# Residual adds regrouped by step, loads reordered, and the closing check spread over three engines in a chunked recurrence

## The chip, the cores and the metric

The kernel runs on one core of one Trainium2 chip. The metric is the device time of one execution, in microseconds (us). The core has five engines that run side by side and wait for one another through semaphores: PE (matrix products), DVE (element-wise work and reductions), ACT (activation functions), POOL (more element-wise work) and SP (here: only starts transfers). "PEld" is PE's loading of weights. Transfers (DMAs) run on 16 DMA engines that all queues share; nearly all of them are started by SP and belong to the queue q1.

## The reference, cut to what matters

The input is x, 4 batches of 128 channels and 4096 tokens (64 x 64). Layer 0 adds a full attention to x, layer 1 adds a causal attention, and then comes the part that the change touches:

```
Wx = layernorm(t) @ W.T                      # t: 4 x 4096 tokens x 128 channels
Wx = (Wx - mean) * rsqrt(var + eps) * gamma + beta     # mean, var over all 4 x 4096 tokens
y = 0
for n in range(4096):                        # one recurrence along the tokens of a batch
    y = sigmoid(Wx[:, n] + y @ V.T)
    ys[:, n] = y
t = t + ys
```

The result t is returned with channels first.

## The kernel before, in words

**The attention layers** (all but the last 60 us of the span) are not touched by the change. At their end the tensor t of each batch lies in DRAM scratch: x2c holds batches 0 and 1 by channels, x2t holds batches 2 and 3 by tokens. These are the "by-channel" batches (b < BY_C = 2) and the "by-token" batches. The last piece of x2t is written at L872, near the end of the last attention block. The projected inputs Wx of the recurrence lie on the chip in xs.

**The recurrence** is cut into chunks. Each batch's 4096 tokens are split into NCH = 256 chunks of STEPS = 16 tokens, and all 256 chunks of a batch advance together: one state tile has 128 channels on the partitions and 256 chunks along the free axis. A chunk doesn't know the state that it should start from. So it first runs over some tokens of the chunk ahead of it (three early steps inside the attention stage, then WARM = 6 steps numbered -6 to -1), which brings it near the right state; that warmed state is kept in the tile start. Then come the 16 real steps, 0 to 15. So there are 22 rounds of 4 batches in this stage.

**One step of one batch** (function step) is a chain over three engines: a product y_ps = V.T x previous state on PE (L1294, which the profile shows as two MATMULs), an add z = Wx x scale + y_ps on DVE (L1296), and a sigmoid on ACT (L1300) that writes the state. The next step of the same batch needs that state. The four batches are independent of each other, so the engines work on the others while one batch's chain is under way.

**The residual** t + ys is added in two ways:

- By-channel batches: add(s) on POOL (L1307) adds the states of batches 0 and 1 of step s to the tile xc (the reloaded x2c), and SP writes the sum out (L1309, 256 KB, pieces of 1 KB). The tile sum has three buffers.
- By-token batches: residual(s0, b, h) takes four steps of one half of the chunks of one batch. PE transposes the four 128x128 blocks into one PSUM tile yT_ps (L1328), DVE adds it to the tile xr, which is the reloaded x2t, in place (L1333), and SP writes it out (L1334, 256 KB, pieces of 2 KB). There are 16 such groups. Twelve are called inside the loop, one in each step from step 4 on, after batch 1's step. Most of the states that they take there are older than the step just before; only the groups called in steps 4, 8 and 12 also take batch 2's state of the step just before, as their fourth block. Four groups are left for after the loop.

**The closing check** (function meet): the last state of a chunk must agree with the warmed start of the next chunk. PE forms the difference with two products, by the identity and by minus the identity (L1317, L1318), ACT squares it twice and sums along the chunks (L1320, L1321). One such pass is made for each of the 4 batches, interleaved with the four remaining residual groups. Then DVE compares the sums with TOL to the fourth power (L1361), counts (L1362), PE adds the counts over the partitions (L1364), and DVE writes a flag (L1367). All engines read the flag (L1424) and branch (L1425): if a check failed, a slow general path would run. With these inputs it doesn't. After the branch SP waits for the landing of all its transfers, and the program ends.

**The order of the work.** A scheduler orders each engine's instructions by when it estimates them to be ready. pin(instruction) (keep_in_program_order) forbids that for one instruction: it comes after whatever the program issued on the same engine just ahead of it. In the kernel before, the step's instructions are pinned from step 4 on, of a residual group the first transpose, the DVE add and the output transfer are pinned, and the loads of xc and xr are not. On each engine instructions start in that order.

**The loads** of this stage are issued on SP: first xc in 8 DMAs of 512 KB (L1249), then xr in 4 DMAs of 1 MB (L1259). xr is read from step 4 on, a quarter of it (one batch, one half) for each group; xc from step 0 on, all 8 parts for each sum.

**PSUM.** Each batch has one buffer for its products (ps_y), and the transposed groups have four (ps_r). [...]

Of the kernel before, what the change touches and what calls it, by code (L numbers as in the profile page):

```python
# [9 lines left out]
F32 = mybir.dt.float32  # L10
AF = mybir.ActivationFunctionType
# [349 lines left out]
def fast_path(  # L361
# [878 lines left out]
    with tc.tile_pool(name="xr", bufs=1) as xrp, tc.tile_pool(name="y", bufs=2) as yp, tc.tile_pool(  # L1240
        name="sums", bufs=3
    ) as sums, tc.tile_pool(
        name="ps_r", bufs=4, space=PSUM
    ) as ps_r, tc.tile_pool(name="ps_y", bufs=1, space=PSUM) as ps_y:

        xc = xrp.tile([P, BY_C, NCH, STEPS], F32, name="xc")
        for b in range(BY_C):
            for c in range(Q):
                nc.sync.dma_start(  # L1249
                    out=xc[ts(c, S), b].rearrange("r (g k) s -> r g (k s)", g=NB),  # L1250
                    in_=x2c[b, :, :, c].rearrange("g r n -> r g n"),
                )
# [4 lines left out]
        for b in range(B - BY_C):  # L1257
            for h in range(HALVES):
                nc.sync.dma_start(out=xr[:, b, h], in_=by_chunk(x2t)[b, h])  # L1259
# [12 lines left out]
        assert HALVES * TPB == NB  # L1272
# [3 lines left out]
        def states(b, s):  # L1276
            if b < BY_C:
                return by_step[:, b, s]
            return pair(early[:, b - BY_C, s]) if s < TPB else late[:, b, s // TPB - 1, s % TPB]

        def step(b, s):
# [4 lines left out]
            order = pin if s >= TPB else lambda ins: None  # L1286
# [25 lines left out]
        gap = xrp.tile([P, B], F32, name="gap")  # L1312

        def meet(b):
            ps = ps_y.tile([P, NCH], F32, tag=f"y{b}", name="gap_ps")
            shaped = grid if b < BY_C else pair
            pin(nc.tensor.matmul(shaped(ps), lhsT=ident, rhs=prev[b], start=True, stop=False))  # L1317
            nc.tensor.matmul(ps, lhsT=minus, rhs=start[:, b, 1:], start=False, stop=True)  # L1318
            sq = yp.tile([P, NCH], F32, tag=f"y{b}", name="sq")
            nc.scalar.activation(sq, ps, AF.Square)  # L1320
            nc.scalar.activation(sq, sq, AF.Square, accum_out=gap[:, b : b + 1])  # L1321


        def residual(s0, b, h):

            ps = ps_r.tile([P, TPB, P], F32, tag="r", name="yT_ps")
            for j in range(TPB):
                ins = nc.tensor.transpose(ps[:, j], states(b, s0 + j)[:, h], ident)  # L1328
                if not j:
                    pin(ins)  # L1330
            part = ds(s0, TPB)
            t = xr[:, b - BY_C, h, part]
            pin(nc.vector.tensor_tensor(t, t, ps, ALU.add))  # L1333
            pin(nc.sync.dma_start(out=by_chunk(out_t)[b - BY_C, h, :, part], in_=t))  # L1334


        groups = [(s0, b, h) for s0 in range(0, STEPS, TPB) for b in range(BY_C, B) for h in range(HALVES)]
        assert HALVES * (B - BY_C) == TPB
        for s in range(-WARM, STEPS):
            for b in range(B):  # L1340
                step(b, s)
                if b == 1 and s >= TPB:
                    group = groups.pop(0)
                    residual(*group)
            if 0 <= s < STEPS - 1:
                add(s)
        tc.mark_branch_hint_location(BRANCH, "LikelyTaken", engines=mybir.ALL_ENGINES)
        for k, group in enumerate(groups):
            residual(*group)
            if k == 1:  # L1350
                add(STEPS - 1)
            if k:
                meet(k - 1)
        meet(B - 1)
# [4 lines left out]
        def judge():  # L1359
            total = xrp.tile([P, 1], F32, name="total")  # L1360
            tc.keep_in_program_order(nc.vector.tensor_scalar(count[:, :B], gap, TOL**4, None, ALU.is_le))  # L1361
# [70 lines left out]
```

## Time and profile before

| what | us |
|---|---|
| median of the 3 timed runs (2019.7 to 2020.23) | 2019.79 |
| the profiled execution, its own time | 2020.46 |
| its span, first to last instruction | 2018.7 |
| first product of the recurrence's 22 rounds (L1294) | from 1961.60 |
| transposes of the first residual group (L1328) | from 1981.97 |
| end of the last sigmoid (L1300) | 2008.75 |
| the comparison that closes the check (L1361) | 2014.47 |
| end of the flag (L1367) | 2015.36 |
| last issue of an output transfer (L1334) | 2012.50 |

The page of the profile gives busy times and the chain that ended last for the whole span; the attention layers fill 97% of it. What the change touches lies in the last 60 us, so the views to read are the timeline and the chain in order of time for that window. In a line of the timeline, the first number is the start in us, the second how long the group of instructions lasts from its first start to its last end, then come engine, source line, operation, out<-in and the shape, a count, and in brackets the idle time ahead of it with what ended it. Ends of MATMULs are modelled by the profiler. A line of the chain in order of time has the start, the time that the chain spent there, and the engine, tile and line.

### The profile page before, as it was taken

The numbers are of one execution on the slowest core, as the hardware profiler recorded it, in microseconds if no ns is written. First come the engines' busy times: TensorE is split into PE (matmuls) and PEld (weight loads), VectorE is DVE, ScalarE is ACT, GpSimd is POOL, SyncE is SP. The second block draws the span as 40 slices with busy tenths as digits, with TensorE's granted clock in tenths as the row PEclk, the third lists the DMA queues.
The fourth block names the chain that finished last, engine by engine and source line by source line (L and its number), as shares of the span: only waits on it lengthen the run. The fifth ranks groups of instructions, "written<-read, shape, count | busy, mean of one in ns | idle before, by whom it ended". The sixth has DMA issues, their size and how long they took to land.

```text
span 2018.7 us, 31252 instructions
## 1 busy us (share of the span) xinstructions
PE 2008.4 (99%) x11888; PEld 876.3 (43%) x11888; DVE 1455.7 (72%) x2811; ACT 975.5 (48%) x1057; POOL 139.8 (7%) x238
## 2 busy tenths in 40 slices
PE   9999999999999999999999999999999999999998
PEld 3333354444333345444433334444433333544457
DVE  4799977554789987655588997655478898764568
ACT  4666633333666653333366664333356665333247
POOL 1000011000000001000000001000000000110014
PEclk9999999999999999999999999999999999999999
DMA  3111112220110111330112111231010111120038
GB/s 105 44 33 23 22 33 50 61 53 16 43 49 18 23 23 37 74 69 16 43 21 60 23 19 32 53 79 37 16 43 2 23 22 23 33 53 16 16 78 278
DMA packets 238443, 89.02 MB, mean 44 GB/s; under 512 B 174816, under 2 KB 219360, under 8 KB 237776
## 3 DMA queue, kind: packets, MB, share of 16 engines
q1 hardware_dynamic: 237280, 86.42, 18.1%
q8 instruction: 94, 1.54, 0.3%
q14 instruction: 61, 0.50, 0.1%
q0 software_dynamic: 288, 0.39, 0.1%
q10 hardware_dynamic: 720, 0.16, 0.0%
HBM read 45.84 MB, written 36.89 MB: 41 GB/s over the span
## 4 chain that ended last, share of the span: by engine, by line
PE 97%; DVE 2%; ACT 1%; issue 0%; POOL 0%; POOLq 0%; DVEq 0%; ACTq 0%
PE s_ps L1017 23%; PE acc L1075 22%; PE s_ps L1004 22%; PE acc L1066 22%; PE o_ps L673 1%; PE kr_ps L562 1%; PE r_ps L624 1%; PE wx_ps L938 1%; DVE z L1296 1%; PE v_ps L574 1%; PE o_ps L685 1%; PE y_ps L1294 1%; DVE xr L1333 0%; PE warm_ps L524 0%; ACT xs L1300 0%; ACT p L1011 0%
## 5 line engine op out<-in xcount | busy, mean ns | idle before, releaser
L1046 DVE TENSOR_TENSOR dsum<-dsum,p 128x1024 f32<-128x1024 f32 x692 | 845.4, 1222 | 403.1 <-ACT p L1020 295.3
L1011 ACT ACTIVATE p<-s_ps,nshift 128x1024 f32<-128x1024 f32 x512 | 569.6, 1116 | 312.9 <-PE s_ps L1004 295.5
L1020 ACT ACTIVATE p<-s_ps 128x1024 f32<-128x1024 f32 (+2 forms) x288 | 274.2, 952 | 601.8 <-PE s_ps L1017 576.7
L1066 PE MATMUL acc<-p,v 64*64 64x512 f32 x4096 | 530.0, 589 | 0.0
L1004 PE MATMUL s_ps<-kr,swap 64*64 64x512 f32 x2048 | 524.6, 590 | 1.3 <-ACT p L1011 1.3
L1004 PE MATMUL s_ps<-kr 64*64 64x512 f32 x2048 | 522.3, 590 | 0.0
L1017 PE MATMUL s_ps<-rows,xhT 128*128 128x512 f32 (+3 forms) x1152 | 500.7, 558 | 0.0
L1075 PE MATMUL acc<-p,xh 128*128 128x512 f32 (+3 forms) x1152 | 500.2, 557 | 0.0
L1017 PEld LDWEIGHTS s_ps<-rows,xhT 128*128 128x128 f32 x1152 | 214.9, 190 | 244.8 <-issue 202.9
L1075 PEld LDWEIGHTS acc<-p,xh 128*128 128x128 f32 x1152 | 216.1, 190 | 239.8 <-issue 223.4
L1066 PEld LDWEIGHTS acc<-p,v 64*64 64x64 f32 x4096 | 156.9, 133 | 283.2 <-issue 274.8
L1004 PEld LDWEIGHTS s_ps<-kr,swap 64*64 64x64 f32 x2048 | 141.8, 133 | 145.7 <-issue 136.0
L1004 PEld LDWEIGHTS s_ps<-kr 64*64 64x64 f32 x2048 | 141.5, 133 | 135.6 <-issue 134.1
L713 POOL TENSOR_TENSOR ln_rstd<-ln_var,mhalf 128x4 f32<-128x4 f32 x64 | 69.9, 1092 | 1186.0 <-DVE ln_var L711 1186.0
L1054 DVE TENSOR_TENSOR dsum<-dsum,p 128x256 f32<-128x256 f32 (+1 forms) x120 | 56.2, 501 | 60.0 <-POOL p L1026 60.0
L699 DVE SCALAR_TENSOR_TENSOR xs<-o_ps,recs,xs 128x128 f32<-128x128 f32 x256 | 70.5, 343 | 5.4 <-PE o_ps L685 1.7
L729 DVE TENSOR_SCALAR xh<-xs,ln_mv,ln_rstd 128x128 f32<-128x128 f32 x252 | 70.2, 342 | 1.9
L708 DVE BATCH_NORM_STATS2 ln_st<-xs 128x6 f32<-128x128 f32 x256 | 62.8, 272 | 0.0
L1026 POOL TENSOR_SCALAR_AFFINE_SELECT p<-p 128x128 f32<-128x128 f32 x128 | 34.5, 294 | 351.9 <-ACT p L1020 347.7
L1044 DVE COPY dsum<-p 128x1024 f32<-128x1024 f32 x44 | 30.2, 686 | 24.7 <-ACT p L1020 15.2
L743 DVE STREAM_TRANSPOSE sqT<-xh 128x512 f32<-128x512 f32 x63 | 44.7, 710 | 1.7
L943 ACT COPY xs<-wx_ps 128x512 f32<-128x512 f32 x31 | 18.1, 584 | 50.4 <-DVE stats L939 48.4
(161 smaller groups left out, 898.3 us busy)
## 6 DMA issues: line engine op xcount, KB each, us to landing
xs<-in_xT SPq DMA_DIRECT2D x32, 256.0 KB, 3.2
by_r<-sqT SPq DMA_DIRECT2D x128, 64.0 KB, 2.2
xhT<-by_r SPq DMA_DIRECT2D x128, 64.0 KB, 2.0
by_c<-sqT SPq DMA_DIRECT2D x124, 64.0 KB, 1.8
xhT<-by_c SPq DMA_DIRECT2D x31, 256.0 KB, 2.8
xs<-in_x SPq DMA_DIRECT2D x12, 512.0 KB, 5.4
swap<-kr SPq DMA_DIRECT2D x32, 128.0 KB, 2.3
x2c<-sqT SPq DMA_DIRECT2D x64, 64.0 KB, 2.3
```

What stands on the lines that cost most here:

```text
L699: nc.vector.scalar_tensor_tensor(t, in0=op[:, ts(j, P)], scalar=rec[:, j : j + 1], in1=t, op0=ALU.mult, op1=ALU.add)
L708: nc.vector.bn_stats(st[:, j], xs[:, b, ds(g * BLK + j * P, P)])
L713: nc.gpsimd.tensor_tensor(y, var, mhalf, ALU.pow)
L729: nc.vector.tensor_scalar(dst[:, j], xs[:, b, ds(g * BLK + j * P, P)], mv[:, j, 0:1], y[:, j : j + 1], ALU.subtract, ALU.mult)
L1004: nc.tensor.matmul(ps[c * M : c * M + M, ts(r, BLK)], lhsT=keys[:, ts(c, M)], rhs=rows[r], start=True, stop=True,)
L1011: nc.scalar.activation(it.p, ps, AF.Exp, bias=nshift)
L1017: nc.tensor.matmul(ps[:, off : off + n], lhsT=lhsT, rhs=rhs, start=True, stop=True)
L1020: ins = nc.scalar.activation(it.p[:, :off], ps[:, :off], AF.Exp, scale=float(P) ** -0.5)
L1046: nc.vector.tensor_tensor(flat, flat, it.p, ALU.add)
L1054: nc.vector.tensor_tensor(den[:, h, q0:], den[:, h, q0:], it.p[:, o : o + n], ALU.add)
L1066: nc.tensor.matmul(bt.acc[c * M : c * M + M, r], lhsT=bt.v[part, m * TPB + j, h], rhs=it.p[part, ts(c, BLK)], start=it.first, stop=it.last,)
L1075: ins = nc.tensor.matmul(bt.acc[:, 0, q0:], lhsT=bt.xh[:, t], rhs=it.p[:, o : o + n], start=it.first and h == 0, stop=it.last and h == 1,)
```

## The change

- xr is loaded ahead of xc, and both sets of loads are pinned.
- A residual group is now one step of both by-token batches and both halves: four transposes (batch 2 half 0, batch 2 half 1, batch 3 half 0, batch 3 half 1) of step s into one PSUM tile, one DVE add of the same size as before, and two output transfers of 128 KB (one per batch) in pieces of 512 bytes. Group s-1 is called in step s, after batch 1's step, from step 1 on. Fifteen groups lie inside the loop and one after it.
- The step's instructions are pinned from step 1 on.
- ps_r has three buffers; the freed PSUM bank holds the new tile met. In steps 4 and 5 ACT copies the warmed starts of batches 2 and 3 into it.
- The check is shared: batches 0 and 1 get their difference from PE, batches 2 and 3 from a DVE subtraction (away); the fourth powers of batches 0 and 3 are summed on ACT, the largest absolute differences of batches 1 and 2 are found on DVE. The comparison is made with the tile tol, which holds TOL to the fourth power or TOL.

```diff
@@ -1240,23 +1240,25 @@
     with tc.tile_pool(name="xr", bufs=1) as xrp, tc.tile_pool(name="y", bufs=2) as yp, tc.tile_pool(
         name="sums", bufs=3
     ) as sums, tc.tile_pool(
-        name="ps_r", bufs=4, space=PSUM
-    ) as ps_r, tc.tile_pool(name="ps_y", bufs=1, space=PSUM) as ps_y:
-
-        xc = xrp.tile([P, BY_C, NCH, STEPS], F32, name="xc")
-        for b in range(BY_C):
-            for c in range(Q):
-                nc.sync.dma_start(
-                    out=xc[ts(c, S), b].rearrange("r (g k) s -> r g (k s)", g=NB),
-                    in_=x2c[b, :, :, c].rearrange("g r n -> r g n"),
-                )
+        name="ps_r", bufs=3, space=PSUM
+    ) as ps_r, tc.tile_pool(name="ps_m2", bufs=1, space=PSUM) as ps_m2, tc.tile_pool(name="ps_y", bufs=1, space=PSUM) as ps_y:
 
         HALVES = NCH // P
         by_chunk = lambda t: t.rearrange("b (h q s) c -> b h q s c", q=P, s=STEPS)
         xr = xrp.tile([P, B - BY_C, HALVES, STEPS, P], F32, name="xr")
         for b in range(B - BY_C):
             for h in range(HALVES):
-                nc.sync.dma_start(out=xr[:, b, h], in_=by_chunk(x2t)[b, h])
+                pin(nc.sync.dma_start(out=xr[:, b, h], in_=by_chunk(x2t)[b, h]))
+
+        xc = xrp.tile([P, BY_C, NCH, STEPS], F32, name="xc")
+        for b in range(BY_C):
+            for c in range(Q):
+                pin(
+                    nc.sync.dma_start(
+                        out=xc[ts(c, S), b].rearrange("r (g k) s -> r g (k s)", g=NB),
+                        in_=x2c[b, :, :, c].rearrange("g r n -> r g n"),
+                    )
+                )
 
         mv = xrp.tile([P, nc.vector.BN_AGGR_DIM], F32, name="mv")
         nc.vector.bn_aggr(mv, ends)
@@ -1269,7 +1271,7 @@
 
-        assert HALVES * TPB == NB
+        assert HALVES * TPB == NB and HALVES * (B - BY_C) == TPB
         early = xrp.tile([P, B - BY_C, TPB, NCH], F32, name="early")
         late = xs.rearrange("p b (r h k q) -> p b k r h q", h=HALVES, r=TPB, q=P)
 
@@ -1283,7 +1285,7 @@
             wx = by_step[:, b, s % STEPS]
             shaped = (lambda t: t) if s < 0 else grid if b < BY_C else pair
 
-            order = pin if s >= TPB else lambda ins: None
+            order = pin if s >= 1 else lambda ins: None
             if s == -1:
                 y = start[:, b, 1:]
             elif s < 0:
@@ -1309,56 +1311,72 @@
             tc.keep_in_program_order(nc.sync.dma_start(out=out_c[:, :, s].rearrange("b c k -> c b k"), in_=t))
 
-        gap = xrp.tile([P, B], F32, name="gap")
-
-        def meet(b):
-            ps = ps_y.tile([P, NCH], F32, tag=f"y{b}", name="gap_ps")
-            shaped = grid if b < BY_C else pair
-            pin(nc.tensor.matmul(shaped(ps), lhsT=ident, rhs=prev[b], start=True, stop=False))
-            nc.tensor.matmul(ps, lhsT=minus, rhs=start[:, b, 1:], start=False, stop=True)
-            sq = yp.tile([P, NCH], F32, tag=f"y{b}", name="sq")
-            nc.scalar.activation(sq, ps, AF.Square)
-            nc.scalar.activation(sq, sq, AF.Square, accum_out=gap[:, b : b + 1])
-
-        def residual(s0, b, h):
+        def residual(s):
 
             ps = ps_r.tile([P, TPB, P], F32, tag="r", name="yT_ps")
             for j in range(TPB):
-                ins = nc.tensor.transpose(ps[:, j], states(b, s0 + j)[:, h], ident)
+                ins = nc.tensor.transpose(ps[:, j], states(BY_C + j // HALVES, s)[:, j % HALVES], ident)
                 if not j:
                     pin(ins)
-            part = ds(s0, TPB)
-            t = xr[:, b - BY_C, h, part]
-            pin(nc.vector.tensor_tensor(t, t, ps, ALU.add))
-            pin(nc.sync.dma_start(out=by_chunk(out_t)[b - BY_C, h, :, part], in_=t))
-
-        groups = [(s0, b, h) for s0 in range(0, STEPS, TPB) for b in range(BY_C, B) for h in range(HALVES)]
-        assert HALVES * (B - BY_C) == TPB
+            t = xr[:, :, :, s]
+            pin(nc.vector.tensor_tensor(t, t, ps.rearrange("p (b h) c -> p b h c", h=HALVES), ALU.add))
+            for b in range(B - BY_C):
+                pin(nc.sync.dma_start(out=by_chunk(out_t)[b, :, :, s].rearrange("h q c -> q h c"), in_=t[:, b]))
+
+        met = ps_m2.tile([P, BY_C, NCH], F32, name="met")
+        gap = xrp.tile([P, B], F32, name="gap")
+        tol = xrp.tile([P, B], F32, name="tol")
+        nc.gpsimd.memset(tol, TOL)
+        nc.gpsimd.memset(tol[:, 0:1], TOL**4)
+        nc.gpsimd.memset(tol[:, B - 1 :], TOL**4)
+
         for s in range(-WARM, STEPS):
             for b in range(B):
                 step(b, s)
-                if b == 1 and s >= TPB:
-                    group = groups.pop(0)
-                    residual(*group)
+                if b == 1 and s >= 1:
+                    residual(s - 1)
+            if TPB <= s < TPB + BY_C:
+                b = s - TPB
+                pin(nc.scalar.copy(met[:, b], start[:, BY_C + b, 1:]))
             if 0 <= s < STEPS - 1:
                 add(s)
+
+        def difference(b):
+            ps = ps_r.tile([P, BLK], F32, tag="r", name="gap_ps")[:, :NCH]
+            pin(nc.tensor.matmul(grid(ps), lhsT=ident, rhs=prev[b], start=True, stop=False))
+            pin(nc.tensor.matmul(ps, lhsT=minus, rhs=start[:, b, 1:], start=False, stop=True))
+            return ps
+
+        def fourths(b, d):
+            sq = yp.tile([P, NCH], F32, tag=f"y{b}", name="sq")
+            pin(nc.scalar.activation(sq, d, AF.Square))
+            pin(nc.scalar.activation(sq, sq, AF.Square, accum_out=gap[:, b : b + 1]))
+
+        def largest(b, d):
+            pin(nc.vector.tensor_reduce(gap[:, b : b + 1], d, AX.X, ALU.max, apply_absolute_value=True))
+
+        def away(b):
+            d = yp.tile([P, NCH], F32, tag=f"z{b}", name="d")
+            pin(nc.vector.tensor_tensor(pair(d), prev[b], pair(met[:, b - BY_C]), ALU.subtract))
+            return d
+
+        first = difference(0)
+        fourths(0, first)
+        add(STEPS - 1)
+        third, fourth = away(2), away(3)
+        residual(STEPS - 1)
+        second = difference(1)
+        fourths(3, fourth)
+        largest(2, third)
+        largest(1, second)
         tc.mark_branch_hint_location(BRANCH, "LikelyTaken", engines=mybir.ALL_ENGINES)
-        for k, group in enumerate(groups):
-            residual(*group)
-            if k == 1:
-                add(STEPS - 1)
-            if k:
-                meet(k - 1)
-        meet(B - 1)
 
         count = xrp.tile([P, B + 2], F32, name="count")
         nc.vector.tensor_copy(count[:, B:], good)
 
         def judge():
             total = xrp.tile([P, 1], F32, name="total")
-            tc.keep_in_program_order(nc.vector.tensor_scalar(count[:, :B], gap, TOL**4, None, ALU.is_le))
+            tc.keep_in_program_order(nc.vector.tensor_tensor(count[:, :B], gap, tol, ALU.is_le))
             tc.keep_in_program_order(nc.vector.tensor_reduce(total, count, AX.X, ALU.add))
             tp = ps_y.tile([1, 1], F32, tag="y0", name="tp")
             nc.tensor.matmul(tp, lhsT=total, rhs=ones, start=True, stop=True)
```

## The prediction

> **What bounds the kernel now.** I read the page first, then the chain that ended last in order of time, then the timeline of single steps. The page says that the attention layers, which the change leaves alone, are nearly everything:
>
> ```profile
> span 2018.7 us, 31252 instructions
> ...
> PE 97%; DVE 2%; ACT 1%; issue 0%; POOL 0%; POOLq 0%; DVEq 0%; ACTq 0%
> ```
>
> So only the last stage, from 1961.6 us on, can change. The chain in order of time shows who holds it (start, time spent, engine, tile, line):
>
> ```profile
> 1986.76 0.48 DVE z L1296
> 1987.24 0.60 DVE xr L1333
> 1987.84 1.08 DVE z L1296 x3
> ...
> 2007.81 0.52 ACT xs L1300
> 2008.33 0.04 issue
> 2008.38 0.77 PE yT_ps L1328 x5
> 2009.14 0.43 PE gap_ps L1317 x2
> 2009.57 0.43 PE gap_ps L1318 x2
> ```
>
> In a step with a residual group DVE is never idle: four z and one xr. After the last sigmoid PE alternates transposes and differences, and ACT's squares follow. The timeline has the links of one step:
>
> ```profile
> 1986.95 1.89 PE L1294 MATMUL y_ps<-xs,vf 128*128 128x256 f32 x8
> ...
> 1987.16 0.68 DVE L1333 TENSOR_TENSOR xr<-xr,yT_ps 128x512 f32<-128x512 f32 x1
> 1987.76 1.65 DVE L1296 SCALAR_TENSOR_TENSOR z<-xs,all_scale,y_ps 128x256 f32<-128x256 f32 x4
> ...
> 1988.68 0.60 PE L1328 MATMUL yT_ps<-ident,early 128*128 128x128 f32 x4
> ...
> 1989.32 0.68 DVE L1333 TENSOR_TENSOR xr<-xr,yT_ps 128x512 f32<-128x512 f32 x1
> ```
>
> Here xr holds DVE for 0.60 (1987.16 to 1987.76), four z for 1.56, 0.39 each, and a step takes 2.16 (1987.16 to 1989.32). A step without a group takes 1.82: the timeline's sigmoids of one batch follow at that distance (1967.57, 1969.39). That is a batch's own round trip: 0.74 from product to z (1980.78 to 1981.52), 0.52 to the sigmoid, 0.56 to the next product.
>
> **The loop.** Four transposes and one add per group stay, so the work per group is the same. What is new is which states they read. Group s-1 takes batch 3's state of step s-1, and on PE it stands ahead of the products of batches 2 and 3 of step s (the first of them is pinned behind the last transpose). On DVE its add stands ahead of their two z. That closes a ring: xr, then z of batch 2, z of batch 3, its sigmoid, two transposes, the next xr. Its links:
>
> - xr holds DVE 0.60, z of batch 2 another 0.39.
> - z of batch 3 to its sigmoid 0.50 (1987.76 to the sigmoid at 1988.26).
> - sigmoid to PE 0.56 (1980.22 to 1980.78).
> - two transposes to xr 0.45: one alone took 0.36 (2008.38 to xr at 2008.74), a second starts 0.11 later (three intervals in 0.60 less the 0.27 of one).
>
> The sum is 2.50 per step, 0.34 over DVE's 2.16. DVE waits, and with it everything. A second row agrees: the group of step 8 already takes batch 2's state of step 7. Its sigmoid ran from 1990.43 to 1990.94, its transpose came at 1991.17, so it had 0.19 to spare. Batch 3's sigmoid ends 0.40 later, and one more transpose follows: 0.40 + 0.11 - 0.19 = 0.32 late. The products behind the transposes don't add to it: batch 2's product starts 0.22 after the first of the two, its z could start 0.74 later, 0.96, while xr frees DVE at 0.45 + 0.60 = 1.05.
>
> From batch 2's z in step 1 to that in step 15, before: 3 x 1.82, 0.60 for the first xr, 11 x 2.16 = 29.8. After: 14 x 2.50 = 35.0, and the first xr in step 1 costs 0.7. The last sigmoid moves by **+5.9**. With each link off by some hundredths (period 2.44 to 2.60) that is +5.0 to +7.3.
>
> [...] If DVE could take the z behind a waiting xr, the step would stay at 2.16 and the last sigmoid would move by 1 only; the trace shows no overtaking, but it has no such wait in the loop either.
>
> **The copies into met** are two on ACT, in steps 4 and 5. ACT works 4 x 0.43 of 2.50, and the copy (0.38 to 0.51, the rows of square and sigmoid) falls after batch 3's sigmoid, where batch 0's next has about 0.5 of slack: 0. If that cover is gone, 1. The three memsets of tol lie on POOL, which waits 4.1 ahead of L489: 0. Three buffers of ps_r in place of four: each is free one group later, 0. The added pins of steps 1 to 3 keep the order that the timeline already shows: 0, at most a few tenths either way.
>
> **The tail.** Before, the last sigmoid ends at 2008.75 and the comparison starts at 2014.47: 5.72. After, with E the end of that sigmoid:
>
> - PE: the difference of batch 0 (0.87) runs ahead of E. The transposes of batch 3 end so that DVE may start at E+0.49; the difference of batch 1 follows, +0.87, ready at E+1.4.
> - DVE: two subtractions (not in the trace of before; 0.39 as z, which also reads one input from PSUM; bounds 0.15 of the smallest operations and 0.60 of xr), the second from E+0.04; xr to E+1.1; two reductions of 128x256 (bounds 0.16, the 128x6 reduction L1362, and 0.67, the 128x512 reduction L637; I take half of the latter, 0.34) to E+1.8.
> - ACT: two squares and their read take 0.93 (2010.04 to 2010.97). Batch 0's run to E+0.85, batch 3's to E+1.8.
>
> The comparison starts at about E+1.85, in place of E+5.72: **-3.9**. With the ends of the bounds it is -3.2 to -4.2. Comparison, count, flag, branch and the waits behind it are as before, 4.2 from 2014.47 to 2018.7. By this path the end moves by 5.9 - 3.9 = +2.0.
>
> **The loads.** SP issued the last piece of x2t at 1954.68; the xr loads now come behind it. Two answers on DMA, 1980 to 1985 (xr's) and 1960 to 1965 (xc's), show both queues full at 417 and 203 GB/s:
>
> ```profile
> DMA packets 288, 2.08 MB, mean 417 GB/s; under 512 B 32, under 2 KB 34, under 8 KB 34
> ```
>
> ```profile
> DMA packets 528, 1.02 MB, mean 203 GB/s; under 512 B 32, under 2 KB 32, under 8 KB 528
> ```
>
> 4.2 MB each: xr takes 10 and xc 21. From 1955.1, or 1957.2 if they wait for that piece to land (2.5), xr is there by 1968, ahead of step 1 (about 1976): 0. xc is there at 1986 to 1989; before, POOL's first sum started at 1976.75. I take 1987.5.
>
> **The stores.** SP issues all in program order, sum 0 first, so every store waits for 1987.5. Before, POOL stood still from 1981.3 to 1988.16 anyway. Sixteen rounds follow. POOL needs 1.51 for one (12.05 for 8 at 1988.16). SP needs 0.37 + 2 x 0.45 = 1.27. The DMA engines: a 512-byte packet cost 26 ns of one engine (the window 1828 to 1831: 528 packets, 28.8% of 16 engines x 3 us), and the mix of 1 KB and 2 KB pieces from 1992 to 2000 moved 21.8 bytes per ns and engine (2.73 MB in 97.8% of 16 x 8). Half of 0.52 MB by each: (13.3 + 12.0) / 16 = 1.58 per round, 25.3 in all, to 2013. The loop ends at 2014.7, so the backlog is gone by then.
>
> [...]
>
> At the end xr of step 15 is done at E+1.2, its two stores are issued by E+2.15 and land 2.5 later, E+4.65. Before, the last store was issued at 2012.50 and landed about when the flag was written, so the trace can't say how much must follow a landing: between 0 and the 3.3 from flag to end. I take 1.7, from the last of SP's waits behind the branch (L1425, at 2017.0) to the end. Then the end lies at E+6.35; it was E+9.95. So stores give 5.9 - 3.6 = +2.3, slightly later than the flag's path, and that decides.
>
> **Sum:** +2.3 on the profiled execution's 2020.46 (span 2018.7 and 1.8 around it), 2022.8. That execution lies 0.67 above the median of the runs shown, so I forecast 2019.79 + 2.3 = **2022.1**, slower by 0.11%. About 0.2%, 4.0 us, is what a measurement of this kernel can tell from no change.
>
> **Rivals.**
>
> 1. *The ring doesn't hold* (the transposes don't wait, or the links overlap). For it: DVE needs only 2.16. Against: products, z, xr and sigmoids are all pinned in program order. The loop then costs three more steps with a group, +1.0; the flag's path would give -2.9, but the stores land at about 2016 and give the end at 2017.5: -1.2, **2018.6**, down to -2.9 (2016.9) if the loads are early.
> 2. *The stores become the end* (slower). Place: q1 behind the late xc. It decides when the start plus 16 rounds passes about 2018.7, that is a round of 1.95 from 1987.5. For it: packets of 512 bytes have only the one uncontended row, and the queue ran 97.8% full already with larger ones; against: 26 ns is far from the 40 it would need. At 52 ns, twice the row, a round is 2.4 and the end +8; I price it at 2.2, landing at 2023.3, the end at 2025: **2026.1**.
> 3. *The check doesn't get shorter*, because its reductions stand behind xr and ACT behind DVE: only the loop's part stays, +5.9: **2025.7**.
>
> **Chances.** Forecast 0.70: within 0.2% 0.56, slower 0.13 (a period above 2.6), faster 0.01. Rival 1 0.12: within 0.10, faster 0.02. Rival 2 0.12: slower 0.11, within 0.01. Rival 3 0.06, slower. That makes faster 0.03, same 0.67, slower 0.30. The range 2017.9 to 2025.7 takes in most of rival 1 and of the forecast's upper tail.
>
> **What would show it.** The distance from xr to xr: 2.50 with DVE idle about 0.35 ahead of xr, waiting for yT_ps (right), 2.16 without idle time (rival 1). The comparison 1.85 behind the last sigmoid. POOL's first sum at 1986 to 1989, and 1.5 to 1.6 from sum to sum. The last landing before 2020. What would make it wrong: a scheduler's order other than the program's on PE or DVE, or xr's loads late in step 1.

## The result and the profile after

| | before | after |
|---|---|---|
| median, same chip, 17 runs each (us) | 2019.84 | 2023.51 |
| profiled execution, its own time | 2020.46 | 2023.69 |
| its span | 2018.7 | 2021.9 |
| first z of the recurrence's 22 rounds, start | 1962.82 | 1962.37 |
| end of the last sigmoid | 2008.75 | 2014.90 |
| comparison that closes the check, start | 2014.47 | 2016.88 |
| end of the flag | 2015.36 | 2017.67 |

The ratio is 1.002, interval 1.0013 to 1.0027: 3.7 us more. That is inside the 0.2% (4.0 us) that the prediction calls no change, but the whole interval lies above 1, so the change is slower rather than equal. In the profiled executions the loop got 6.6 us longer, measured from its own start, and the check 3.7 us shorter; 0.9 us came after the flag. Together with a stage that began 0.45 earlier and a flag that follows its comparison 0.1 sooner that is 3.2; the profiled execution of before lies 0.6 above its median, that of after 0.2, which is the rest of the 3.7. Two of the 17 executions after took longer than all others, 2025.18 and 2027.73. Of all executions reported below one, of w1, took 3571.34 and counts as slow; w1's ratio leaves it out.

The page still gives the attention layers nearly the whole of the chain that ended last:

```profile
span 2021.9 us, 31279 instructions
...
PE 99%; DVE 0%; ACT 0%; issue 0%; POOL 0%; POOLq 0%; DVEq 0%; ACTq 0%
```

The chain in order of time is another one in the last stage. Before, it ran along DVE (z and xr by turns); now it stays on PE (start, time spent, engine, tile, line):

```profile
1984.78 1.73 PE y_ps L1296 x8
1986.51 0.82 PE yT_ps L1318 x4
1987.33 1.73 PE y_ps L1296 x8
1989.06 0.82 PE yT_ps L1318 x4
...
2014.57 0.84 PE yT_ps L1318 x4
2015.41 0.02 issue
2015.43 0.69 DVE xr L1322
```

One round is 1.73 + 0.82 = 2.55. That PE carries the chain doesn't mean that it works all that time: the timeline of one step shows its weight loads idle and DVE idle ahead of xr (in brackets, with what ended it).

```profile
1979.71 0.69 DVE L1322 TENSOR_TENSOR xr<-xr,yT_ps 128x512 f32<-128x512 f32 x1 [0.30 <-PE yT_ps L1318]
...
1980.32 1.65 DVE L1298 SCALAR_TENSOR_TENSOR z<-xs,all_scale,y_ps 128x256 f32<-128x256 f32 x4
...
1980.83 0.91 ACT L1302 ACTIVATE early<-z,all_shift 128x256 f32<-128x256 f32 x2 [0.84 <-DVE z L1298]
1981.39 0.20 PEld L1318 LDWEIGHTS yT_ps<-ident,early 128*128 128x128 f32 x2 [0.39 <-ACT early L1302]
...
1981.79 0.20 PEld L1318 LDWEIGHTS yT_ps<-ident,early 128*128 128x128 f32 x2 [0.20 <-ACT early L1302]
...
1982.06 1.03 PE L1296 MATMUL y_ps<-early,vf 128*128 128x256 f32 x4
1982.27 0.69 DVE L1322 TENSOR_TENSOR xr<-xr,yT_ps 128x512 f32<-128x512 f32 x1 [0.30 <-PE yT_ps L1318]
```

From xr to xr it is 2.56 here (1979.71 to 1982.27) and 2.55 over the loop. The sigmoids of batches 2 and 3 run one after the other (0.91 for both); the transposes wait for the first (0.39 idle) and again for the second (0.20); xr waits for the transposes (0.30). The view of waits sums it over the stage (us in total, times, longest):

```profile
POOL sum L1309 <- PE y_ps L1296: 27.4, 1, 27.4
...
PEld yT_ps L1318 <- ACT xs L1302: 7.0, 24, 0.4
DVE xr L1322 <- PE yT_ps L1318: 4.4, 15, 0.3
```

Its first line is a wait that the inference names wrongly. POOL's first sum, in POOL's own timeline, starts at 1988.71, 1.0 behind the last packets of xc (the DMA answer for 1986 to 1990 shows traffic until 1987.7 and none after), not behind a product. In the kernel before, the first sum started 12 us earlier (the first line is before, the second after):

```profile
1976.75 4.50 POOL L1307 TENSOR_TENSOR sum<-xs,xc 128x512 f32<-128x512 f32 x3 [15.00 <-ACT xs L1300]
...
1988.71 7.49 POOL L1309 TENSOR_TENSOR sum<-xs,xc 128x512 f32<-128x512 f32 x5 [27.42 <-PE y_ps L1296]
```

After the last sigmoid the check is now short. Five lines of the timeline:

```profile
2014.54 0.82 DVE L1360 TENSOR_TENSOR d<-xs,met 128x256 f32<-128x256 f32 x2 [0.18 <-ACT xs L1302]
...
2016.37 0.41 DVE L1356 TENSOR_REDUCE gap<-gap_ps 128x1 f32<-128x256 f32 x1
...
2016.75 1.07 SPq L1324 DMA_DIRECT2D out_x<-xr  x2
2016.88 0.16 DVE L1379 TENSOR_TENSOR count<-gap,tol 128x4 f32<-128x4 f32 x1
...
2017.52 0.15 DVE L1385 TENSOR_SCALAR flag<-tp 1x1 int32<-1x1 f32 x1 [0.28 <-PE tp L1382]
```

SP still issues stores (to 2017.82) when the flag is written (2017.67). From the flag to the end it is 4.2, before 3.3.

### The profile page after: what moved, and what is told of

It is laid out like the page before. It is cut to its first block, busy times and chain, and to the rows that moved or that the text cites. A ratio compares the mean times of both kernels' runs of the same rounds, so it can differ in the third digit from the quotient of the medians.

```text
span 2021.9 us, 31279 instructions
## 1 busy us (share of the span) xinstructions
PE 2011.8 (100%) x11880; PEld 874.9 (43%) x11880; DVE 1457.4 (72%) x2815; ACT 973.8 (48%) x1053; POOL 140.1 (7%) x241
## 4 chain that ended last, share of the span: by engine, by line
PE 99%; DVE 0%; ACT 0%; issue 0%; POOL 0%; POOLq 0%; DVEq 0%; ACTq 0%
PE s_ps L1017 23%; PE acc L1075 22%; PE s_ps L1004 22%; PE acc L1066 22%; PE y_ps L1296 2%; PE o_ps L673 1%; PE r_ps L624 1%; PE kr_ps L562 1%; PE wx_ps L938 1%; PE v_ps L574 1%; PE o_ps L685 1%; PE yT_ps L1318 1%; PE warm_ps L524 0%; ACT p L1011 0%; PE early_ps L789 0%; PE early_ps L794 0%
```

## The experiments

The theory was the ring: the group called after batch 1's step takes batch 3's state of the step before, so the step grows from 2.16 to 2.55. The rival for the time lost was the late start of the output stores behind xc. Each ratio is against the kernel before on the same chip, with its interval. All kernels do the whole computation. A profile is of one execution. Those of e1, e2 and e3 took 2027.08, 2028.03 and 2027.4, which is 1.7, 4.8 and 2.5 above their medians, so points of time late in these three profiles are later than in a typical execution.

| label | edit | median us | ratio |
|---|---|---|---|
| e1_late_group | change, group after batch 3 | 2025.34 | 1.0027 [1.0017, 1.0037] |
| e2_pair_stores | change, by-token stores per two steps | 2023.27 | 1.0019 [1.001, 1.0028] |
| e3_late_pair | both | 2024.9 | 1.0029 [1.0019, 1.0039] |
| e4_two_queues | change, half of xc on POOL's queue | 2025.83 | 1.0032 [1.002, 1.0044] |
| b1_load_order | before, new load order | 2040.84 | 1.0106 [1.0092, 1.0121] |
| b1b_load_order | the same, branch hint behind the last group | 2024.9 | 1.0025 [1.0015, 1.0034] |
| b2_shared_check | before, shared check | 2018.07 | 0.9992 [0.9983, 1.0001] |
| c1_old_check | change, check of before | 2025.24 | 1.0028 [1.0017, 1.0038] |
| v8_split_sums | e3, xc in two parts, sums per batch | 2019.72 | 1.0001 [0.9992, 1.001] |
| w0_wide_loads_ring | change, xc loaded by 128 partitions | 2022.91 | 1.0016 [1.0007, 1.0025] |
| w1_wide_loads | e1, xc loaded by 128 partitions | 2017.13 | 0.9988 [0.9979, 0.9996] |
| w3_wide_pair | w1, stores per two steps | 2017.27 | 0.9987 [0.9978, 0.9996] |

**Is it the ring?** The group is called one place later in the program, after batch 3's step instead of batch 1's; nothing else changes.

```diff
-                if b == 1 and s >= 1:
+                if b == B - 1 and s >= 1:
                     residual(s - 1)
```

> The changed kernel, with the residual group of step s-1 called after batch 3's step instead of after batch 1's, so that its transposes stand behind the products of batches 2 and 3, which need the same states; nothing else is altered. Theory ring: the step of 2.55 us comes from transposes and add waiting for batch 3's fresh state ahead of two products and two z; here the wait is gone, the step falls to DVE's 2.16, and the last sigmoid comes 5 to 5.5 us earlier, at about 2009.5. Rival stores: the output transfers, 16 rounds of 1.6 us from 1990, end at about 2017 whatever the loop does, so the time falls by less than 1 us, to 2022.7 to 2023.5. If the loop alone set the end, the time would be near 2018. Both may hold: the step shortens and the time hardly moves.

DVE's timeline in e1 has no idle time left, and xr follows xr at 2.165:

```profile
1989.12 0.68 DVE L1322 TENSOR_TENSOR xr<-xr,yT_ps 128x512 f32<-128x512 f32 x1
1989.72 1.65 DVE L1298 SCALAR_TENSOR_TENSOR z<-xs,all_scale,y_ps 128x256 f32<-128x256 f32 x4
1991.29 0.68 DVE L1322 TENSOR_TENSOR xr<-xr,yT_ps 128x512 f32<-128x512 f32 x1
1991.89 1.65 DVE L1298 SCALAR_TENSOR_TENSOR z<-xs,all_scale,y_ps 128x256 f32<-128x256 f32 x4
1993.45 0.68 DVE L1322 TENSOR_TENSOR xr<-xr,yT_ps 128x512 f32<-128x512 f32 x1
```

So the ring is shown: one line moved, and the last sigmoid ends 5.6 us earlier (at 2009.27, the flag at 2012.14). Yet the time didn't fall; 2025.34 lies above all that was expected. SP's timeline, with the flag long written, goes on issuing stores one after the other:

```profile
2014.25 2.16 SPq L1324 DMA_DIRECT2D out_x<-xr  x2
2016.50 0.42 SPq L1311 DMA_DIRECT2D out_x<-sum  x1
2017.01 1.01 SPq L1324 DMA_DIRECT2D out_x<-xr  x2
2018.11 0.46 SPq L1311 DMA_DIRECT2D out_x<-sum  x1
2018.66 1.00 SPq L1324 DMA_DIRECT2D out_x<-xr  x2
2019.75 0.46 SPq L1311 DMA_DIRECT2D out_x<-sum  x1
2020.30 1.01 SPq L1324 DMA_DIRECT2D out_x<-xr  x2
```

First sum at 1990.39, first store at 1991.96, last store issued at 2021.31: the ring had hidden a second limit of nearly the same length.

**Is it the pieces of 512 bytes?** The by-token stores wait for two steps and go out as 256 KB in pieces of 1 KB, alone (e2) and with e1's edit (e3).

```diff
-            for b in range(B - BY_C):
-                pin(nc.sync.dma_start(out=by_chunk(out_t)[b, :, :, s].rearrange("h q c -> q h c"), in_=t[:, b]))
+            for b in range(B - BY_C if s % 2 else 0):
+                part = ds(s - 1, 2)
+                pin(nc.sync.dma_start(out=by_chunk(out_t)[b, :, :, part].rearrange("h q s c -> q h s c"), in_=xr[:, b, :, part]))
```

> The changed kernel, with the by-token stores made once per two steps and batch (256 KB in pieces of 1 KB) instead of once per step and batch (128 KB in pieces of 512 bytes); the placement of the group stays. Theory ring: the loop keeps its 2.55 us per step, the last sigmoid stays at about 2014.9. Theory small pieces: a round of stores falls from 1.62 to POOL's 1.51 or so, SP has no backlog at the end, and the distance from the flag to the end shrinks from 4.2 to 3.3: 2022.6. Rival: SP and the queue are not what stretches the end; then the time stays at 2023.5.

> The changed kernel with both edits: the group after batch 3's step, and the by-token stores once per two steps in pieces of 1 KB. Theory ring plus stores: the last sigmoid at about 2009.5, the flag's path would end at 2015.5, and the stores, which can't start before 1989 because xc comes late, end about 16 x 1.53 later; end near 2018, time 2019 to 2020, about the kernel before. If only the loop counted: 2017. If the stores' start counted most, it can't fall below 2019.

e2 stands at 2023.27, as the change, with its ring whole (2.55). e3 missed: 2024.9. Its loop is short (last sigmoid 2008.79, flag 2012.36), but the first sum started at 1991.35 and the last store was issued at 2021.17. With larger pieces POOL's 1.5 per sum takes the queue's place as the pace, so sixteen rounds from 1991 end past 2015 anyway, and two pauses are added. Larger pieces gain nothing that can be told from none, with the ring (e2) or without it (e3). What is left is the late start; w1 below tests it.

**Is the late xc a matter of its queue?** Half of xc's loads are issued by POOL.

```diff
-                    nc.sync.dma_start(
+                    (nc.sync if c < Q // 2 else nc.gpsimd).dma_start(
```

> The changed kernel, with half of xc's loads (the parts that go to the partitions 64 to 127) issued on POOL's queue instead of SP's; the rest stays. The xc loads alone ran at 205 GB/s with all engines busy while xr ran at 417. Theory: two queues let the parts for the two halves of the partitions interleave, xc lands 5 to 10 us earlier, POOL's first sum starts at 1979 to 1984 instead of 1988.7, the stores have no backlog at the end, and the end falls to the flag's path: 2022.6. The loop stays at 2.55. Rival: the rate of xc doesn't depend on the queue, and nothing moves. POOL's issue of four transfers ahead of the variance's power could also delay the stage's start by up to 4 us: up to 2027.

It isn't, as far as this run goes. The first sum started at 1989.94, no earlier than in the change, and the time rose to 2025.83, for which no run shows the reason. The DMA answer for 1970 to 1975:

```profile
DMA packets 239, 1.35 MB, mean 270 GB/s; under 512 B 22, under 2 KB 22, under 8 KB 126
...
q1 hardware_dynamic: 119, 0.93, 67.7%
q0 software_dynamic: 120, 0.43, 31.7%
```

The two queues share the 16 engines (67.7 and 31.7% of their time). But SP's queue (q1) still carries xr there, in packets of nearly 8 KB on average, while POOL's queue (q0) brings its half of xc; so xr's packets pass until about 1975, in the change until about 1966.5. From 1976 to 1980 both queues carry xc, and the rate is 282 GB/s, above the 209 of the change in the same stretch. What the second queue gained there it had taken from xr.

**What is the load order worth alone?** The kernel before with xr's loads ahead of xc's, both pinned, and nothing else of the change.

```diff
-        xc = xrp.tile([P, BY_C, NCH, STEPS], F32, name="xc")
-        for b in range(BY_C):
-            for c in range(Q):
-                nc.sync.dma_start(
...
-                nc.sync.dma_start(out=xr[:, b, h], in_=by_chunk(x2t)[b, h])
+                pin(nc.sync.dma_start(out=xr[:, b, h], in_=by_chunk(x2t)[b, h]))
+
+        xc = xrp.tile([P, BY_C, NCH, STEPS], F32, name="xc")
+        for b in range(BY_C):
+            for c in range(Q):
+                pin(
```

> The kernel before with one part of the change alone: xr loaded ahead of xc, both pinned. Theory stores: POOL's sums can't start before 1988 to 1991 instead of 1976.75; 16 sums of 1.51 us and a stall of 1 to 2 us (SP and the queue paused for that long in every run so far, at a 16 KB packet on the instruction queue) end at 2014 to 2017, so the last store is issued 2 to 4 us later than 2012.5, and the end moves by +1 to +3: 2020.5 to 2022.5. Rival: before, the stores stood still until 1988 anyway behind xr's loads, so nothing moves: 2019.6. The loop keeps 2.16 us per step in both.

2040.84 says nothing of the load order: the scheduler now puts two late by-token stores ahead of all stores of sums on SP, and the sums' stores stand behind them until 2008. SP's waits:

```profile
SPq L1336 <- DVE xr L1335: 38.4, 2, 38.3
```

b1b is the same kernel with the branch hint behind the last group, which leaves SP in the program's order.

```diff
-        tc.mark_branch_hint_location(BRANCH, "LikelyTaken", engines=mybir.ALL_ENGINES)
         for k, group in enumerate(groups):
...
         meet(B - 1)
+        tc.mark_branch_hint_location(BRANCH, "LikelyTaken", engines=mybir.ALL_ENGINES)
```

> As b1_load_order (the kernel before with xr loaded ahead of xc, both pinned), with the branch hint traced behind the last group, so that SP keeps the stores in the program's order; in b1_load_order two late stores stood ahead of all sums on SP and held them until 2008. Theory stores: first sum at 1988 to 1991, 16 sums and one pause of 1 to 2 us, last store 2 to 4 us later than 2012.5: 2020.5 to 2022.5. Rival: the stores before were held until 1988 by xr's loads anyway: 2019.7.

2024.9: the load order costs 5 us, more than expected (what the hint's place does by itself no run shows). There is no ring (2.17 from xr to xr) and the flag is written at 2014.62, earlier than before the change; but the first sum starts at 1988.78, the last store is issued at 2016.4, and its landing is what SP waits for until about 2020.8.

**What is the shared check worth alone?** The kernel before with met, tol and the four new functions, its groups as they were.

```diff
...
+        first = difference(0)
+        fourths(0, first)
+        second = difference(1)
+        add(STEPS - 1)
+        third, fourth = away(2), away(3)
+        largest(1, second)
+        for group in groups[:2]:
+            residual(*group)
+        fourths(3, fourth)
+        largest(2, third)
         tc.mark_branch_hint_location(BRANCH, "LikelyTaken", engines=mybir.ALL_ENGINES)
-        for k, group in enumerate(groups):
+        for group in groups[2:]:
             residual(*group)
-            if k == 1:
-                add(STEPS - 1)
-            if k:
-                meet(k - 1)
-        meet(B - 1)
```

> The kernel before with the shared check alone (PE, ACT and DVE), the four remaining residual groups still behind the loop, and ps_r with three buffers. Theory: the comparison comes about 4.1 us behind the last sigmoid instead of 5.7, because four groups of transposes and adds remain; the end moves by -1.2 to -1.6, limited by the last stores: 2018.0 to 2018.5. Rival: the last stores, not the flag, already set the end of the kernel before; then the time stays at 2019.6.

> The changed kernel with the check of the kernel before: four differences by PE and the fourth powers of all four batches on ACT, behind the loop and the last residual group; ps_r again with four buffers, no copies in steps 4 and 5. Theory: the loop keeps its 2.55 us per step and the last sigmoid stays at 2014.9; the comparison comes 4.5 to 5 us behind it instead of 2.0 (four differences of 0.87 on PE behind the transposes, the last batch's squares, 0.9, behind them), the flag near 2020.5, the end 3.3 to 3.6 behind that: 2025 to 2026. Rival: the stores set the end of the change and hide the check; then it stays at 2023.5 to 2024.5.

2018.07 against 2019.72: 1.65 us less. The other way round, the change with the old check (c1: meet called for all four batches behind the last residual) took 2025.24, 1.7 more than the change, both as expected. c1's timeline shows what the sharing avoids, ACT's squares of four batches in a row (the last two batches here), with DVE idle 3.72 ahead of the comparison:

```profile
2017.05 0.38 ACT L1342 ACTIVATE sq<-gap_ps 128x256 f32<-128x256 f32 x1
...
2017.47 0.42 ACT L1343 ACTIVATE sq<-sq 128x256 f32<-128x256 f32 x1
...
2017.92 0.38 ACT L1342 ACTIVATE sq<-gap_ps 128x256 f32<-128x256 f32 x1
...
2018.33 0.42 ACT L1343 ACTIVATE sq<-sq 128x256 f32<-128x256 f32 x1
...
2018.87 0.17 DVE L1356 TENSOR_SCALAR count<-gap 128x4 f32<-128x4 f32 x1 [3.72 <-ACT sq L1343]
```

**Can the stores start earlier?** v8 loads batch 0's half of xc first, then xr, then the other half, and makes POOL's sums per batch (128x256, 0.82 to 0.87 each), so that half of the output needn't wait.

```diff
+        load_xc(0)
+        for b in range(B - BY_C):
+            for h in range(HALVES):
+                pin(nc.sync.dma_start(out=xr[:, b, h], in_=by_chunk(x2t)[b, h]))
+        load_xc(1)
```

> The kernel of e3_late_pair (group after batch 3's step, by-token stores in pairs of steps), with the loads ordered xc of batch 0, xr, xc of batch 1, and the by-channel sums made and stored per batch (128x256, 128 KB), batch 1's following later. Theory: batch 0's sums can start near 1975 while the other loads still run, so that less is left for after 1988; the stores end at 2012 to 2014 and the end at 2016 to 2018: time 2017 to 2019.5. Rival: the queue is full with loads until 1988 anyway, all stores still have to follow, 8.4 MB at 300 to 340 GB/s, 25 to 28 us: end at 2017 to 2020, time 2019 to 2022. The last sigmoid at 2009.3 in both.

2019.72, level with the kernel before, as the rival said: first sum at 1974.77, last store issued by 2013.74, but xr came late (first at 1980.40) and the last sigmoid ended at 2011.36. The loads of xc keep the shape that passes at half of xr's rate in the change (206 GB/s from 1970 to 1975, xr 424 from 1960 to 1965); only the order was traded.

w1 takes that half rate away. So far each load of xc went to 32 partitions; with the scratch x2c laid out by channel block, each load fills all 128. Each write of x2c in the attention stage becomes four smaller ones. w1 has e1's edit as well, w0 has not, w3 adds e2's stores to w1.

```diff
-    x2c = dram.tile([BY_C, NB, S, Q, BLK], F32, name="x2c")
+    x2c = dram.tile([BY_C, NB, Q, S, BLK], F32, name="x2c")
...
                 for q in range(Q):
...
+                    for c in range(Q):
+                        nc.sync.dma_start(out=to[c, :, :, q], in_=sq[ts(q, S), c])
...
-            for c in range(Q):
+            for g in range(0, NB, 2):
                 pin(
                     nc.sync.dma_start(
-                        out=xc[ts(c, S), b].rearrange("r (g k) s -> r g (k s)", g=NB),
-                        in_=x2c[b, :, :, c].rearrange("g r n -> r g n"),
+                        out=xc[:, b, ds(g * CPB, 2 * CPB)].rearrange("p (g k) s -> p g (k s)", g=2),
+                        in_=x2c[b, g : g + 2].rearrange("g c r n -> (c r) g n"),
```

> The kernel of e1_late_group, with the scratch x2c laid out so that one load fills all 128 partitions (8 loads of 512 KB with 32 partitions each become 8 loads of 512 KB with 128 partitions each); in return each of the 64 stores into x2c during the attention layers becomes four smaller ones. Theory: xc's 205 GB/s come from its shape (32 partitions a load, rows 8 KB apart); at xr's 417 it lands by 1978, POOL's sums start 10 us earlier, the stores are done with the loop, and the end is the flag's path behind a last sigmoid at 2009.3: 2016.5 to 2018, faster than before by 1.5 to 3. Rival 1: the rate is that of 2 KB reads whatever the shape: then 2024 to 2025.5 as e1_late_group. Rival 2: the added stores on SP delay the attention layers: above 2025.

> The changed kernel with the wide xc loads of w1_wide_loads alone; the residual group stays after batch 1's step. Theory ring plus stores: xc lands by 1979 and the stores keep up with the loop, but the step stays at 2.55 us and the last sigmoid at 2014 to 2015: the end is the flag's path, 3.3 to 3.6 behind the flag, 2020.5 to 2021.3, time 2022 to 2022.8, some 1 us better than the change. If the late stores were what the change lost, it would fall to 2017 as w1_wide_loads.

> The kernel of w1_wide_loads with the by-token stores once per two steps in pieces of 1 KB. Theory: there the end is the flag's path behind a last sigmoid at 2008.3 to 2009.3, the stores are done in time, so larger pieces change nothing: 2017.1. Rival: the last two stores of 128 KB and SP's issue of them set the end; then the last stores, now 256 KB each, make it 0.3 to 0.6 slower or faster.

The DMA answer of the change for 1970 to 1975, when xc is on its way (packets, bytes, mean rate, packets by size):

```profile
DMA packets 534, 1.03 MB, mean 206 GB/s; under 512 B 32, under 2 KB 32, under 8 KB 534
```

The same stretch of w1:

```profile
DMA packets 1002, 1.94 MB, mean 387 GB/s; under 512 B 57, under 2 KB 57, under 8 KB 1002
```

The packets are of the same size, 2 KB, and the queue is full in both; a packet takes 158 ns of an engine in the change (105.5% of 16 x 5 us over 534) and 84 in w1 (104.6% over 1002). POOL's timeline in w1 starts 9.5 us earlier:

```profile
1979.24 7.52 POOL L1307 TENSOR_TENSOR sum<-xs,xc 128x512 f32<-128x512 f32 x5 [18.53 <-PE y_ps L1294]
```

w1 took 2017.13, less than both kernels: step 2.165, last sigmoid 2008.27, flag 2011.15. The stores are level with the loop; SP issues the last one before the flag is written:

```profile
2009.84 1.01 SPq L1322 DMA_DIRECT2D out_x<-xr  x2
...
2011.00 0.15 DVE L1383 TENSOR_SCALAR flag<-tp 1x1 int32<-1x1 f32 x1 [0.28 <-PE tp L1380]
```

w3 is within 0.2 of it: with the stores on time, larger pieces gain nothing. Together with the change and e1 these make a table of two causes (median, us):

| | xc late (32 partitions) | xc early (128 partitions) |
|---|---|---|
| group after batch 1 (ring) | change 2023.51 | w0 2022.91 |
| group after batch 3 (no ring) | e1 2025.34 | w1 2017.13 |

Taking away one cause gains nothing that these runs can tell from none: the intervals of w0 and of e1 both overlap the change's. (w0's median is 0.6 lower, near the 0.9 that the stores add behind the flag in the change.) Taking away both gains 6.4. With the stores early, the place of the group alone moves the ratio from 1.0016 [1.0007, 1.0025] to 0.9988 [0.9979, 0.9996], 5.8 us between the medians.

e1's median even lies 1.8 above the change's, though its stores had no reason to be later. Two things are seen in the profiled executions: xc was there 1.7 later (first sum 1990.39 against 1988.71; 0.4 of it because the stage began later), and two pauses of the stores fell into e1, one into the change. At each pause one store's issue takes 1.4 to 1.9 instead of 0.5 (1.91 for two in the change at 2000.95, 2.46 and 2.16 in e1 at 1997.59 and 2014.25, elsewhere 1.0). At the pause of the change and the second of e1 a 16 KB packet of the instruction queue q8 passes (2001.3 and 2014.5, 1.2 and 1.4 us of an engine). In the change the next such packet comes near 2020.2, behind the stores; in e1, whose loop ends earlier, near 2014.5, and POOL loses 1.65 waiting for a store. That fits, but no run changed when those packets come, so it isn't shown as the cause.

## Why the prediction held, point by point

**The ring** was right in mechanism and a little short in size. Its five links, in the step from 1984.82 on: xr to z 0.60 (0.60 predicted), z to the next z 0.40 (0.39), z to sigmoid 0.52 (0.50), sigmoid to PE 0.55 (0.56), two transposes to xr 0.48 (0.45). Their sum is 2.55, not 2.50. Over fourteen steps that is +0.7, so the loop grew by 6.6 instead of 5.9. DVE's wait ahead of xr is 0.30; 0.35 was predicted.

**DVE's order** was given too much. The prediction said that with overtaking on DVE the step would stay at 2.16. The trace shows no overtaking (no z starts in the 15 waits ahead of xr, 4.4 us in all); but it also shows that overtaking would have gained next to nothing. Batch 2's product stands behind batch 3's transposes on PE and starts at 1987.17; with the 0.74 from product to z its z could start at 1987.91, and it did at 1987.97. So PE's order closes a second ring: z 0.40, sigmoid 0.52, transposes 0.55, product 0.28, z 0.74, together 2.49. It takes both orders to be changed, as e1's one line does. No run changed DVE's order alone, so the 2.49 is worked out and not measured.

**Copies into met, memsets, three buffers, pins: 0.** One copy stands at 1986.74 between two sigmoids, and the step with it is 2.55 as the others.

**The tail.** With E the end of the last sigmoid, the comparison starts at E+1.98; predicted E+1.85. A subtraction holds 0.41 (0.39 taken), a reduction 0.41 of which 0.33 lie ahead of the next (0.34). The tail term is -3.74, not -3.9. Rival 3 (the check doesn't get shorter) is out: in time the shared check alone is worth 1.65 (b2) and 1.7 (c1). That is less than the 3.74 of the tail. With the old groups behind the loop the comparison comes at E+3.73 (b2) instead of E+5.72; with the new ones the old check has it at E+4.94 (c1) and the shared one at E+1.98. So of the 3.74 the check is 2.0 to 3.0 and the moved groups are the rest; and in c1 the stores land before the flag, so the 0.9 that they add in the change falls away there.

**The loads.** xc was put at 1986 to 1989 and POOL's first sum at 1987.5; the last packets passed at 1987.7 and the sum started at 1988.71. xr is there in time: its first add, in step 1, waits 0.21, for the transposes.

**The stores** were the step that failed. The prediction had the backlog gone by 2013, ahead of the loop's end; SP issues one store after the other to 2017.82, behind the flag. Of these 5.0 us, 1.2 are the later start and 1.6 the first sum itself, which has to be made before a store can be issued and was left out. The other 2.2 are the rounds, sixteen in 27.5 instead of 25.3: a round took 1.65 instead of 1.58 (SP's stores of the sums from 2004.64 to 2016.20, seven rounds in 11.56), and a pause near 2002 cost about 0.9, one store's issue of 1.40 instead of 0.5. The price of a packet was right. The change's DMA answer for 1992 to 2000, with the share of 16 engines in its second line:

```profile
DMA packets 3877, 2.44 MB, mean 305 GB/s; under 512 B 232, under 2 KB 3876, under 8 KB 3876
...
q1 hardware_dynamic: 3876, 2.43, 100.6%
```

w3's for 1984 to 1990, with pieces of 1 KB alone:

```profile
DMA packets 2100, 2.03 MB, mean 338 GB/s; under 512 B 119, under 2 KB 2100, under 8 KB 2100
...
q1 hardware_dynamic: 2100, 2.03, 102.3%
```

w3 gives 46.8 ns of an engine per packet of 1 KB. In the change two packets in three have 512 bytes; 128.8 us over 3876 packets, less a third of them at 46.8, leaves 26.4 ns for one, where 26 was taken. Two of these, 52.8 ns, cost 13% more than one of 1 KB. What was missing were the first sum, the late start, the pause and that the queue has no room to catch up in: it was full. The end came at E+7.0 (E+6.35 predicted).

**The sum** for the profiled execution: -0.45 for an earlier start of the stage, +6.6 for the loop, -3.74 to the comparison, -0.10 from there to the flag, +0.88 from flag to end, together +3.2, as the span. Predicted was +2.3. The ring gave +0.7 of the difference, the stores +0.6 (0.3 of the 0.88 were forecast), the tail about +0.1, and the earlier start took 0.45 back. That start lies anywhere from 1961.40 (c1) to 1962.82 (before) in the profiles of these kernels, so this part of the agreement is luck.

**The rivals.** Rival 1 (the ring doesn't hold) is out by 2.55 and by e1. Its price was wrong too: a loop without the ring was put at 2018.6, and e1, which is that case, took 2025.3. The reason is rival 2, the stores, which was tied to one condition, a round of 1.95 or more. It needed no such round: in e1 rounds of 1.70 (eight from 2000.14 to 2013.71), a first sum at 1990.39 and two pauses were enough. In the change itself the stores set only the last 0.9. The two rivals were priced one at a time, each with the other cause as forecast, and that is the weak place: what was hidden behind the ring got no number.

## What to carry to other kernels

When a consumer is moved nearer to its producer, write down the ring that it closes over all engines' queues, link by link, and compare it with the busiest engine's work per step; here one line's place was worth 0.39 us in each of 14 steps. Before a limit is removed, price the next one behind it: removing the ring alone, or the late loads alone, gained nothing, and both together beat both kernels. An order of loads is a promise about the first consumer of the last one; ask when the stores behind it start and whether their queue has room to catch up.

## What the runs showed of the hardware

- **Partitions per load.** A load into 32 partitions ran at 206 GB/s with a full queue, the same bytes in the same 2 KB packets into 128 partitions at 387. The ratio is 0.53. In e4, where two queues carry xc to different halves of the partitions from 1976 to 1980, the rate was 282 GB/s against 209 in the change; but the packets differ too, on POOL's queue there 3.5 KB on average (0.80 MB in 228, from 1975 to 1985), on SP's 1.9 (1.52 MB in 782), and the first sum started no earlier (1989.94 against 1988.71). The layout in DRAM changed with the shape of the load (the rows of neighbouring partitions lay 8 KB apart before, 2 KB in w1), and no run separates the two.
- **Instruction packets.** One 16 KB packet of the instruction queue took 0.96 us of an engine (before, 1998 to 2000) to 1.5 (e1, 2013.5 to 2017.5). Where it fell into a full store queue, one store's issue took 1.4 us (change) and 1.65 (e1) instead of 0.5, and the rate then dropped from about 300 GB/s to 20 to 128 for 0.7 us (change, from 2002.7) and to 31 to 51 for 0.9 (e1, from 2016.0).
- **The end.** From SP's wait for the last landing to the end it is 2.0 in the change (2019.84 to 2021.87) and 1.8 in e4 (2021.55 to 2023.32); the prediction took 1.7. From the flag to the end, with no store late, it is 3.3 (before, w0, c1) to 3.8 (w3).
